# Graph attention on one core: units of six tiles instead of quads, one PSUM place for each product, sums copied by VectorE

## Chip, cores, metric

The kernel runs on one core of a Trainium2 chip. The metric is the device time of one execution in microseconds (us). The engines are named as in the profile: PE (TensorE; PEld is its weight load), DVE (VectorE), ACT (ScalarE), POOL (GpSimd), SP (SyncE).

## The reference

6250 nodes with 128 features, 206,250 edges sorted by receiver, with two sets of 32 edge features and a weight each. Everything is float32. `senders` is the input `src`, `receivers` is `dst`.

```python
w_ij = jax.nn.silu(edge_feats @ rad_W1 + rad_b1) @ rad_W2 + rad_b2
w_ij = w_ij + (jax.nn.silu(chi_scalar @ sph_W1 + sph_b1) @ sph_W2 + sph_b2)
q_i = (node_feats @ Wq).reshape(-1, 8, 16)[receivers]
k_j = (node_feats @ Wk).reshape(-1, 8, 16)[senders]
alpha = (q_i * w_ij * k_j).sum(axis=-1) / jnp.sqrt(16.0)
alpha = alpha * cutoffs[:, None]
v_j = (node_feats @ Wv)[senders].reshape(-1, 8, 16)
out = jax.ops.segment_sum(alpha[..., None] * v_j, receivers, num_segments=n_nodes) / 16.0
x = _layernorm(x + out.reshape(-1, 128), axis=-1)
```

## The kernel before

**Tiling.** 128 edges are a tile, four tiles a quad, four quads (16 tiles) a group. There are 1612 tiles, 403 quads and 101 groups. The receivers of a quad lie within 32 node rows, those of a group within 128.

**Start.** `load_nodes`, `turn` and `k_and_v` make keys and values of all nodes (x times Wk and Wv) and write them to a table in DRAM, `kv_tab`. Meanwhile GpSimd gathers rows of x for the first ten quads (`gather_x`, `XQ`), whose keys and values are computed directly. `tables`, `receivers` and others prepare row numbers.

**A quad in the main loop.** GpSimd gathers 128 rows of `kv_tab` per tile (`gathers`, line 131, through the helper at line 120), 14 quads ahead (`AHEAD`) into a ring of 16 (`RING`). TensorE computes the two hidden layers (`hidden_of`, line 405, tile `ph`), ScalarE applies silu (line 440, tile `act`); TensorE spreads the queries to the edges with a one-hot matrix (`q_at_edges`, line 413, `pq`) and computes the weights w_ij (`weigh`, line 447, `pw`: one product for the bias, line 450, then eight at line 455). VectorE multiplies queries by keys (`multiply`, line 463), by the weights (line 471), reduces over the head (473), scales (475), and multiplies the values (`messages`, 486). TensorE sums messages over the receivers of a quad with the one-hot matrix `hot` (`sum_quads`, line 492, `po`).

**A group.** `pick` and `turn_q` (line 378) fetch and transpose the x rows of the receivers, `make_q` (388) makes their queries; ScalarE copies both out of PSUM. `part_sums` (527) copies the sums of a group, `sum_group` (532 and 534) places them with the one-hot matrices `to` that `place` (521, 522) makes, and adds the rest of the group before (`tot`, copied at 536). `statistics` computes mean and variance (548 to 551), and every fourth group `roots` and `normalize` (556 to 570) finish rows, which SP writes.

**Order.** It is written out by hand: each engine runs its instructions in the program's order. The loop at line 624 takes a quad per turn, with TensorE one quad ahead of VectorE and the hidden layers two ahead. `ph`, `pq` and `pw` have two places in PSUM each (one bank a place), `po` and `side` one. `add_manual_dep` calls add waits: each gather waits for its own `pw` matmul of an earlier quad (line 137), and most steps of VectorE and ScalarE for marks of TensorE (`after`, `behind`). The last three quads are written out from line 681.

Of the kernel before, what the change touches and what calls it, by code (L numbers as in the profile page):

```python
# [44 lines left out]
XQ = 10  # L45
RING = 16
# [8 lines left out]
def gnn_kernel(ctx, tc, x, src, dst, weight, edges, rad_W1, rad_b1, rad_W2, rad_b2,  # L55
# [26 lines left out]
    src_x = const.tile([P, math.ceil(XQ / NQ) * GT], I32, name="src_x")  # L82
# [31 lines left out]
    alphas = side[:, 2 * P:2 * P + QT * HEADS].rearrange("p (t h) -> p t h", h=HEADS)  # L114

    def quad_of(name, bufs, width=D):
        return ep.tile([P, QT, width], F32, name=name, bufs=bufs)
# [8 lines left out]
    order = [g * NQ + j for g in range(NG) for j in (0, 2, 1, 3) if g * NQ + j < QUADS]  # L126
# [4 lines left out]
    def gathers(q, marks=()):  # L131

        kv = quad_of("kv", RING, 2 * D)
        for t in range(QT):
            o = gather(kv[:, t, :], kv_tab, src_i[:, q * QT + t:q * QT + t + 1])
            if marks:
                tc.add_manual_dep(o.ins, marks[t].ins.name, WAIT, reason="no gather ahead of TensorE")
        kv_of[q] = kv

    def load_feats(g, mark=None):  # L140
        feats_of[g] = gp.tile([P, EG // 2], F32, name="feats")
        o = nc.sync.dma_start(feats_of[g], edges[g])
        if mark is not None:
            tc.add_manual_dep(o.ins, mark.ins.name, WAIT, reason="one signal of TensorE a quad")
# [15 lines left out]
    def load_x(g, mark=None):  # L160
# [4 lines left out]
        o = nc.sync.dma_start(x_of[g].bitcast(U8), rows_from(x, r_of[g]))  # L165
        if mark is not None:
            tc.add_manual_dep(o.ins, mark.ins.name, WAIT, reason="one signal of TensorE a quad")
# [5 lines left out]
    nc.sync.dma_start(src_x, src[:, :math.ceil(XQ / NQ) * GT])  # L173
# [13 lines left out]
    with tc.tile_pool(name="nodes", bufs=1) as nodes, \  # L187
            tc.tile_pool(name="nodes_ps", bufs=2, space=PSUM) as nps:
        chunks = [(c, min(QT, NB - c)) for c in range(0, NB, QT)]
        quads_x = order[:XQ]  # L190
# [8 lines left out]
        def load_nodes(k):  # L199
            c, n = chunks[k]  # L200
            xs = ep.tile([P, EQ], F32, name="act", bufs=8).rearrange("p (t d) -> p t d", d=D)
            xs_of[k] = xs
# [8 lines left out]
        def gather_x(q):  # L211
            xs_of[q, "x"] = xs = quad_of("msg", XQ)
            for t in range(QT):
                gather(xs[:, t, :], x, src_x[:, q * QT + t:q * QT + t + 1])

        def turn(k, n):
            pt = nps.tile([P, QT, P], F32, name="pt", bufs=3)
            for i in range(n):
                nc.tensor.transpose(pt[:, i, :], xs_of[k][:, i, :], ident)
            xT_of[k] = nodes.tile([P, QT, P], F32, name="xT", bufs=4)  # L220
            nc.scalar.activation(xT_of[k][:, :n, :], pt[:, :n, :], AF.Copy)

        def k_and_v(k, n):
            kvs = quad_of("kv", RING, 2 * D)
            for h in range(0, n, 2):
                m = min(2, n - h)
                pk = nps.tile([P, 2, 2 * D], F32, name="pk", bufs=3)
                for i in range(m):
                    nc.tensor.matmul(pk[:, i, :], xT_of[k][:, h + i, :], wkv, start=True, stop=True)
                nc.vector.tensor_copy(kvs[:, h:h + m, :], pk[:, :m, :])  # L230
            return kvs
# [5 lines left out]

        qb = nodes.tile([P, NG, NQ], F32, name="qb")
# [82 lines left out]
        AHEAD = RING - 2  # L321
# [4 lines left out]
        for q in quads_x:  # L326
            gather_x(q)
# [7 lines left out]
        work = [(k, n) for k, (c, n) in enumerate(chunks)] + [((q, "x"), QT) for q in quads_x]  # L335
        turn(*work[0])
        turn(*work[1])
        for i, (k, n) in enumerate(work):
            if i + 2 < len(work):
                turn(*work[i + 2])  # L340
            kvs = k_and_v(k, n)
# [5 lines left out]
            store(k, kvs)  # L347
            if k + 8 < len(chunks):
                load_nodes(k + 8)
            if k == 4:  # L350
                nc.sync.dma_start(src_i, src)
            for f in beside.get(k, []):
                f()
            if i == len(chunks) - 1:
                nc.sync.dma_start(scale, weight)
        for q in order[XQ:AHEAD]:
            gathers(q)
# [5 lines left out]
        nc.vector.tensor_scalar(scale, scale, SCALE, None, op0=OP.mult)  # L363


    with tc.tile_pool(name="ps", bufs=1, space=PSUM) as pp:
# [8 lines left out]
        def turn_q(g):  # L375
            n = quads_in(g)
            pt = pp.tile([P, EQ], F32, name="pq", bufs=2)
            o = nc.tensor.matmul(pt[:, :n * W], x_of[g], pick_of[g][:, :n, :], start=True, stop=True)
            for m in made:
                tc.declare_no_dep(o.ins, m.ins, reason="VectorE has read it")  # L380
            xT_of[g] = gp.tile([P, P], F32, name="xT")
            return lambda: nc.scalar.activation(xT_of[g][:, :n * W], pt[:, :n * W], AF.Copy)

        def make_q(g):

            n = quads_in(g) * W
            pt = pp.tile([P, EQ], F32, name="pq", bufs=2)
            nc.tensor.matmul(pt[:n, :D], xT_of[g][:, :n], wq, start=True, stop=True)  # L388
            q_of[g] = gp.tile([P, D], F32, name="q")
            return lambda: nc.scalar.activation(q_of[g][:n, :], pt[:n, :D], AF.Copy)  # L390
# [12 lines left out]
        def hidden_of(q, i):  # L403

            g, j = divmod(q, NQ)
            r0, c0 = 2 * R * (j // 2) + i * R, EQ * (j % 2)
            act_of[q, i] = pp.tile([P, EQ], F32, name="ph", bufs=2)
            return nc.tensor.matmul(act_of[q, i], w1[r0:r0 + R, :],  # L408
                                    feats_of[g][r0:r0 + R, c0:c0 + EQ], start=True, stop=True)

        made = []

        def q_at_edges(q):
            g, j = divmod(q, NQ)
            b = slice(j * W, (j + 1) * W)
            pq_of[q] = pp.tile([P, EQ], F32, name="pq", bufs=2).rearrange("p (t d) -> p t d", d=D)
            made.clear()
            for t in range(QT):
                o = nc.tensor.matmul(pq_of[q][:, t, :], hotT_of[g][b, t * P:(t + 1) * P],  # L419
                                     q_of[g][b, :], start=True, stop=True)  # L420
                made.append(o)
            return o

        def after(o, mark, reason="one signal of TensorE a quad"):
            tc.add_manual_dep(o.ins, mark.ins.name, WAIT, reason=reason)

        def behind(o, marks, k):

            if marks:
                after(o, marks[k], "a signal of TensorE behind the quad's own")  # L430

        def first_layers(q):

            return [hidden_of(q, i) for i in range(2)][-1]

        def silus(q, mark, marks=()):

            for i in range(2):
                act = ep.tile([P, EQ], F32, name="act", bufs=8)
                o = nc.scalar.activation(act, act_of[q, i], AF.Silu, bias=b1[:, i:i + 1])  # L440
                if i == 0:
                    after(o, mark)
                else:
                    behind(o, marks, 0)
                act_of[q, i] = act

        def weigh(q):

            pw = pp.tile([P, EQ], F32, name="pw", bufs=2)
            nc.tensor.matmul(pw, onesb, brow.rearrange("p t d -> p (t d)"), start=True, stop=False)  # L450
            pw = pw_of[q] = pw.rearrange("p (t d) -> p t d", d=D)
            marks = []
            for t in range(QT):
                for i in range(2):
                    o = nc.tensor.matmul(pw[:, t, :], act_of[q, i][:, t * P:(t + 1) * P], w2[:, i, :],  # L455
                                         start=False, stop=(t == QT - 1 and i == 1))
                    marks.append(o)
            return marks

        def multiply(q, mark=None, t=slice(0, QT)):  # L460
            if t.start == 0:
                kq_of[q] = quad_of("kq", 3)
            o = nc.vector.tensor_tensor(kq_of[q][:, t, :], pq_of[q][:, t, :], kv_of[q][:, t, :D],  # L463
                                        op=OP.mult)
            if mark is not None:
                after(o, mark)

        def scores(q, t=slice(0, QT), marks=()):
            n = t.stop - t.start
            m = kq_of[q][:, t, :]  # L470
            nc.vector.tensor_tensor(m, pw_of[q][:, t, :], m, op=OP.mult)  # L471
            alpha = alphas[:, t, :]
            o = nc.vector.tensor_reduce(alpha, m.rearrange("p t (h e) -> p t h e", e=HD), AX.X, OP.add)  # L473
            behind(o, marks, 1)
            o = nc.vector.tensor_tensor(  # L475
                alpha, alpha,
                scale[:, q * QT + t.start:q * QT + t.stop, None].to_broadcast([P, n, HEADS]),
                op=OP.mult)
# [415 lines left out]
```

## Time and profile before

| | |
|---|---|
| median of 3 runs | 2040.4 us (2038.44 to 2041.47) |
| the profiled execution | 2041.07 us, span 2039.3 us |
| mean granted TensorE clock | 0.922 |
| gathers of `kv_tab`: count, mean duration | 1572, 947 ns |
| DVE operations 128x512 of the main loop, mean | 680 to 694 ns |
| silu 128x512 on ACT, mean | 685 ns |
| HBM read and written | 287.58 and 13.46 MB |

A line of a timeline gives start and duration in us, the engine, the line of the code, the operation, output and inputs with their shapes, the count, and in brackets the idle time of the engine before it and what ended it. A line of groups gives busy time and mean duration in ns, then the idle time before the instructions of the group and its releasers. A line of windows gives busy time of PE, PEld, DVE, ACT and POOL with the number of instructions, the granted clock, the busy share of the DMA engines and GB/s.

### The profile page before, as it was taken

The page shows a single profiled execution, that of the slowest core. Times are in us where ns is not written, and L with a number is a line of the kernel's source. Part 1 is how long each engine was busy: PE and PEld are TensorE (multiplying, and loading weights), DVE is VectorE, ACT ScalarE, POOL GpSimd, SP SyncE. Part 2 cuts the span into 40 slices and gives each one's busy share as a digit, 9 for nine tenths or more (in the row PEclk, how much of TensorE's full clock was granted, in tenths as well). Part 3 has the DMA queues.
Part 4 walks back from the last instruction along what each step waited for, and adds up shares of the span by engine and source line. Part 5 has one row for each costly group of instructions (what it writes and reads, how often), then busy time and mean ns, then how long its engine had stood idle before and what let it go on. Part 6 is the DMA issues. An engine that isn't in the chain of part 4 may idle for free.

```text
span 2039.3 us, 44163 instructions
## 1 busy us (share of the span) xinstructions
PE 1839.6 (90%) x16011; PEld 1525.5 (75%) x16011; DVE 1469.2 (72%) x3008; ACT 719.9 (35%) x1426; POOL 1527.4 (75%) x1620
## 2 busy tenths in 40 slices
PE   9899999898888988898988998889989989899897
PEld 7788887677777776777776776777767777777776
DVE  6688887687777666767777676767767676777677
ACT  2344433333333233333333333332333333333323
POOL 7777777777777777777777777777777777777775
PEclk9899999998898899988999889899999988898898
DMA  8455555455454445454454545454544545454543
GB/s 309 142 154 155 151 153 153 137 152 153 137 151 141 148 143 149 142 149 144 143 153 136 151 141 150 139 153 139 151 142 146 152 137 152 141 148 141 152 145 90
DMA packets 141371, 304.03 MB, mean 149 GB/s; under 512 B 34028, under 2 KB 73820, under 8 KB 141148
## 3 DMA queue, kind: packets, MB, share of 16 engines
q0 software_dynamic: 76736, 208.77, 35.9%
q1 hardware_dynamic: 62912, 92.00, 14.0%
q8 instruction: 127, 2.08, 0.4%
q14 instruction: 96, 0.79, 0.1%
q10 hardware_dynamic: 1500, 0.40, 0.1%
HBM read 287.58 MB, written 13.46 MB: 148 GB/s over the span
## 4 chain that ended last, share of the span: by engine, by line
PE 51%; DMA 20%; DVE 13%; issue 8%; ACT 4%; POOL 4%; DVEq 0%; POOLq 0%; ACTq 0%
PE pw L455 25%; DMA kv<-kv_tab,src_i 19%; PE pq L419 9%; PE ph L408 7%; DVE kq L463 5%; PE po L497 4%; DVE side L473 2%; POOL kv L120 2%; PE pw L450 2%; DVE kq L471 2%; POOL msg L120 2%; ACT L440 2%; ACT y L570 1%; PE pq L388 1%; PE pq L532 1%
## 5 line engine op out<-in xcount | busy, mean ns | idle before, releaser
L120 POOL DMA_INDIRECT kv<-kv_tab,src_i x1572 | 1488.0, 947 | 482.0 <-PE pw L455 188.9
L440 ACT ACTIVATE act<-ph,b 128x512 f32<-128x512 f32 x806 | 518.2, 685 | 1167.8 <-PE pq L419 1150.6
L455 PE MATMUL pw<-w,act 128*128 128x128 f32 x6448 | 906.1, 299 | 0.0
L455 PEld LDWEIGHTS pw<-w,act 128*128 128x128 f32 x6448 | 825.8, 208 | 102.2 <-issue 89.5
L463 DVE TENSOR_TENSOR kq<-pq,kv 128x512 f32<-128x512 f32 x404 | 278.1, 688 | 394.3 <-DMA kv<-kv_tab,src_i 240.0
L408 PE MATMUL ph<-feats,w 32*128 32x512 f32 x1612 | 505.4, 685 | 21.9 <-ACT act L440 21.9
L419 PE MATMUL pq<-q,hotT 32*128 32x128 f32 x3224 | 498.1, 297 | 23.5 <-DVE kq L463 23.0
L419 PEld LDWEIGHTS pq<-q,hotT 32*128 32x128 f32 x3224 | 419.6, 199 | 81.7 <-issue 51.6
L473 DVE TENSOR_REDUCE side<-kq 128x32 f32<-128x512 f32 x404 | 280.2, 694 | 42.0 <-PE pw L455 0.5
L486 DVE TENSOR_TENSOR msg<-kv,side 128x512 f32<-128x512 f32 x404 | 277.5, 687 | 43.8 <-DVE side L475 1.4
L471 DVE TENSOR_TENSOR kq<-pw,kq 128x512 f32<-128x512 f32 x404 | 274.7, 680 | 0.1
L408 PEld LDWEIGHTS ph<-feats,w 32*128 32x128 f32 x1612 | 139.6, 195 | 104.5 <-issue 59.3
L450 PE MATMUL pw<-brow,onesb 3*128 3x512 bf16 x403 | 160.4, 398 | 0.0
L497 PE MATMUL po<-msg,hot 128*32 128x128 f32 x3200 | 156.6, 293 | 0.0
L532 PE MATMUL pq<-part,to 128*128 128x128 f32 x200 | 46.1, 313 | 105.0 <-DVE kq L463 66.9
L532 PEld LDWEIGHTS pq<-part,to 128*128 128x128 f32 x200 | 30.6, 193 | 118.0 <-issue 69.8
L475 DVE TENSOR_TENSOR side<-side,scale 128x32 f32<-128x32 f32 x404 | 80.8, 200 | 42.9 <-DVE side L473 1.4
L497 PEld LDWEIGHTS po<-msg,hot 128*32 128x32 f32 x3200 | 71.8, 112 | 38.6 <-issue 5.0
L388 PE MATMUL pq<-wq,xT 128*128 128x128 f32 (+1 forms) x202 | 47.8, 322 | 32.2 <-DVE kq L463 31.6
L394 DVE TENSOR_TENSOR hotT<-relb,side 128x512 f32<-128x512 bf16 x101 | 68.8, 681 | 0.0
L399 DVE TENSOR_TENSOR hot<-rel,side 128x512 f32<-128x512 f32 x100 | 66.1, 661 | 0.0
L388 PEld LDWEIGHTS pq<-wq,xT 128*128 128x128 f32 (+1 forms) x202 | 35.3, 218 | 40.3 <-DVE kq L463 39.6
(101 smaller groups left out, 831.0 us busy)
## 6 DMA issues: line engine op xcount, KB each, us to landing
feats<-in_edges SPq DMA_DIRECT2D x101, 512.0 KB
kv<-kv_tab,src_i POOLq DMA_INDIRECT x1572
relb<-rel_lin SPq DMA_DIRECT2D x101, 128.0 KB
x<-in_x SPq DMA_DIRECT2D x101, 64.0 KB
out<-y SPq DMA_DIRECT2D x101, 64.0 KB
kv_tab<-kv SPq DMA_DIRECT2D x12, 512.0 KB
act<-in_x SPq DMA_DIRECT2D x12, 256.0 KB
dst_i<-in_dst SPq DMA_DIRECT2D x1, 808.0 KB
```

What stands on the lines that cost most here:

```text
L120: return nc.gpsimd.indirect_dma_start(out=o, out_offset=None, in_=table, in_offset=bass.IndirectOffsetOnAxis(ap=index, axis=0))
L388: nc.tensor.matmul(pt[:n, :D], xT_of[g][:, :n], wq, start=True, stop=True)
L408: return nc.tensor.matmul(act_of[q, i], w1[r0:r0 + R, :], feats_of[g][r0:r0 + R, c0:c0 + EQ], start=True, stop=True)
L419: o = nc.tensor.matmul(pq_of[q][:, t, :], hotT_of[g][b, t * P:(t + 1) * P], q_of[g][b, :], start=True, stop=True)
L440: o = nc.scalar.activation(act, act_of[q, i], AF.Silu, bias=b1[:, i:i + 1])
L450: nc.tensor.matmul(pw, onesb, brow.rearrange("p t d -> p (t d)"), start=True, stop=False)
L455: o = nc.tensor.matmul(pw[:, t, :], act_of[q, i][:, t * P:(t + 1) * P], w2[:, i, :], start=False, stop=(t == QT - 1 and i == 1))
L463: o = nc.vector.tensor_tensor(kq_of[q][:, t, :], pq_of[q][:, t, :], kv_of[q][:, t, :D], op=OP.mult)
L471: nc.vector.tensor_tensor(m, pw_of[q][:, t, :], m, op=OP.mult)
L473: o = nc.vector.tensor_reduce(alpha, m.rearrange("p t (h e) -> p t h e", e=HD), AX.X, OP.add)
L486: o = nc.vector.tensor_tensor(msg_of[q][:, t, :].rearrange("p t (h e) -> p t h e", e=HD), kv_of[q][:, t, D:].rearrange("p t (h e) -> p t h ...
L497: o = nc.tensor.matmul(po_of[g][j * W:(j + 1) * W, :], hot_of[g][:, j * QT + t, :], msg_of[g * NQ + j][:, t, :], start=(t == 0), stop=(t = ...
```

## The change

A unit takes the place of the quad: a quad and half of another one, six tiles. Three quads `a, b, c` of a hand-made order become two units: `a` with the first half of `b`, and `c` with the second half. 269 units cover the 1612 tiles. VectorE's five steps and the gathers go by units; the ring has ten units of kv (60 tiles; before 16 quads, 64 tiles), gathered nine units ahead.

Each product of a unit has its own place in PSUM: `ph` three banks (two layers of the unit's own quad and one of a shared quad), `pq` two (six tiles, `turn_q` and `make_q`), `pw` two (six tiles, the sums of a group and its total). There is one place of each. `behind` makes the first instruction that writes a bank again wait for the bank's last reader.

The first gather of a unit waits for `weigh` of an earlier unit (`past`), the other five do not. The manual waits of VectorE, ScalarE and SP are gone. Four small results of a group (`xT`, `q`, `part`, `tot`) are copied from PSUM by VectorE, not by ScalarE. The sums over the edges of a group are done in one unit (`sums`), the total in the next (`closes`); `place` is a task at the end of the unit of `sums`. `scale` is written in the order of units by 25 small operations. The end of the kernel is written out anew for the last two units.

```diff
-XQ = 10
-RING = 16
+U = 6
+XU = 7
+RING = 10
...
-    order = [g * NQ + j for g in range(NG) for j in (0, 2, 1, 3) if g * NQ + j < QUADS]
+    turn_of_quads = ((0, 0), (0, 1), (0, 2), (1, 0), (0, 3), (1, 2), (1, 1), (2, 0), (1, 3), (2, 1), (2, 2), (2, 3))
+    order = [(b + g) * NQ + j for b in range(0, NG, 3) for g, j in turn_of_quads if (b + g) * NQ + j < QUADS]
+    order[-7:] = [*range((NG - 2) * NQ, (NG - 1) * NQ), QUADS - 1, QUADS - 3, QUADS - 2]
+    units = []
+    for a, *rest in (order[i:i + 3] for i in range(0, len(order), 3)):
+        units.append([a * QT + t for t in range(QT)])
+        if rest:
+            b, c = rest
+            units[-1] += [b * QT, b * QT + 1]
+            units.append([c * QT + t for t in range(QT)] + [b * QT + 2, b * QT + 3])
+    UNITS = len(units)
+    layers = [[(unit[0] // QT, 0), (unit[0] // QT, 1)] for unit in units]
+    for v in range(1, UNITS, 2):
+        b = units[v][-1] // QT
+        layers[max(v - 2, 0)].append((b, 0))
+        layers[v - 1].append((b, 1))
...
+    group_of = [[t // GT for t in unit] for unit in units]
+    first = [min(v for v in range(UNITS) if g in group_of[v]) for g in range(NG)]
+    last = [max(v for v in range(UNITS) if g in group_of[v]) for g in range(NG)]
+    place_of = {t: (v, k) for v, unit in enumerate(units) for k, t in enumerate(unit)}
...
+
+    def gathers(v, mark=None):
+
+        kv = unit_of("kv", RING, 2 * D)
+        for k, t in enumerate(units[v]):
+            o = gather(kv[:, k, :], kv_tab, src_i[:, t:t + 1])
+            if mark is not None and k == 0:
+                tc.add_manual_dep(o.ins, mark.ins.name, WAIT, reason="no gather ahead of TensorE")
+        kv_of[v] = kv
...
-        AHEAD = RING - 2
+        AHEAD = RING - 1
...
-        nc.vector.tensor_scalar(scale, scale, SCALE, None, op0=OP.mult)
+        full = UNITS // 8 * 8
+        for v in list(range(8)) + list(range(full, UNITS)):
+            for k in range(0, len(units[v]), QT):
+                m = min(QT, len(units[v]) - k)
+                i, t = v * U + k, units[v][k]
+                o, w = scale[:, i:i + m], weights[:, t:t + m]
+                if v < 8:
+                    o, w = (a[:, :full * U].rearrange("p (c t) -> p c t", t=8 * U)[:, :, b:b + m]
+                            for a, b in ((scale, i), (weights, t)))
+                nc.vector.tensor_scalar(o, w, SCALE, None, op0=OP.mult)
...
-        def turn_q(g):
+        def turn_q(g, ps):
...
-            pt = pp.tile([P, EQ], F32, name="pq", bufs=2)
+            pt = ps[:, U * D:(U + 1) * D]
...
-        def make_q(g):
+            return o, lambda: nc.vector.tensor_copy(xT_of[g][:, :n * W], pt[:, :n * W])
...
+        def behind(o, *banks):
+
+            for bank in banks:
+                if bank in readers:
+                    after(o, readers.pop(bank), "a bank has one user at a time")
...
+        def q_at_edges(v, part):
+            for k in part:
+                t = units[v][k]
+                g, j = divmod(t // QT, NQ)
+                b = slice(j * W, (j + 1) * W)
+                o = nc.tensor.matmul(tiles_in(pq_of[v], v)[:, k], hotT_of[g][b, t % QT * P:(t % QT + 1) * P],
+                                     q_of[g][b, :], start=True, stop=True)
+                behind(o, "pq%d" % (k // QT))
+
+        def hidden(s, v=None):
+
+            ph = pp.tile([P, 3, EQ], F32, name="ph", bufs=1)
+            for k, (q, i) in enumerate(layers[s][:3]):
+                if v is not None and k == 2:
+                    q_at_edges(v, range(QT))
+                hidden_of(ph, k, q, i)
+            if v is not None:
+                q_at_edges(v, range(len(layers[s][:3]) // 3 * QT, len(units[v])))
+            return ph
...
+        def silu(ps, k, q, i):
+            act = ep.tile([P, EQ], F32, name="act" if k < 2 else "act_b", bufs=4)
+            readers["ph%d" % k] = nc.scalar.activation(act, ps[:, k, :], AF.Silu, bias=b1[:, i:i + 1])
...
+        def weigh(v):
+
+            n = len(units[v])
+            for k in range(0, n, QT):
+                m = min(QT, n - k) * D
+                o = nc.tensor.matmul(pw_of[v][:, k * D:k * D + m], onesb,
+                                     brow.rearrange("p t d -> p (t d)")[:, :m], start=True, stop=False)
+                behind(o, "pw%d" % (k // QT))
...
+        def multiply(v):
+            kq_of[v] = unit_of("kq", 2)
+            n = len(units[v])
+            o = nc.vector.tensor_tensor(kq_of[v][:, :n], tiles_in(pq_of[v], v), kv_of[v][:, :n, :D],
+                                        op=OP.mult)
+            readers["pq0"] = readers["pq1"] = o
+
+        def weigh_scores(v):
+            m = kq_of[v][:, :len(units[v])]
+            o = nc.vector.tensor_tensor(m, tiles_in(pw_of[v], v), m, op=OP.mult)
+            readers["pw0"] = readers["pw1"] = o
...
+        def part_sums(g, po):
+            return nc.vector.tensor_copy(part_of[g][:n, :], po[:n, :])
...
+        def sum_group(g, ph, bank):
             n, part, to = quads_in(g) * W, part_of[g], to_of[g]
-            ph = pp.tile([P, EQ], F32, name="pq", bufs=2)
-            nc.tensor.matmul(ph[:, :D], to[:n, 0, :], part[:n, :], start=True, stop=(g == 0))
+            o = nc.tensor.matmul(ph, to[:n, 0, :], part[:n, :], start=True, stop=(g == 0))
+            behind(o, bank)
...
+        def totals(g, ph):
+            nc.vector.tensor_copy(tot_of[g], ph)
+            return add_x(g, ph)
...
+        turns = {first[g] - 2: g for g in range(1, NG)}
+        makes = {first[g] - 1: g for g in range(1, NG)}
+        sums = {last[g] + 2: g for g in range(G - 1)}
+        closes = {last[g] + 3: g for g in range(G - 1)}
+        for g in range(NG):
+            if first[g] - 4 >= 0:
+                at(first[g] - 4, lambda g=g: pick(g))
+            if g < G:
+                at(first[g] + 2, lambda g=g: one_hots(g))
+                at(min(last[g] + 2, UNITS - 3), lambda g=g: place(g))
+            if g < G - 1:
+                at(last[g] + 3, lambda g=g: statistics(g))
...
+        for v in range(UNITS - 2):
+            pq_of[v] = pp.tile([P, 2 * EQ], F32, name="pq", bufs=1)
+            after_q, after_w = [], []
+            for at_v, f in ((turns, turn_q), (makes, make_q)):
+                if v in at_v:
+                    o, copy = f(at_v[v], pq_of[v])
+                    behind(o, "pq1")
+                    after_q.append(copy)
+            ph = hidden(v + 1, v)
+            pw_of[v] = pp.tile([P, 2 * EQ], F32, name="pw", bufs=1)
+            small = [pw_of[v][:, (U + k) * D:(U + k + 1) * D] for k in range(2)]
+            if v in sums:
+                g = sums[v]
+                sum_quads(g, small[0], "pw1")
+                after_w.append(lambda g=g: part_sums(g, small[0]))
+            if v in closes:
+                g = closes[v]
+                sum_group(g, small[1], "pw1")
+                after_w.append(lambda g=g: totals(g, small[1]))
+            if v == judged:
+                after_w.append(verdict(pw_of[v]))
+            past, mark = mark, weigh(v)
+            silus(v + 1, ph)
+            if v + AHEAD < UNITS:
+                gathers(v + AHEAD, past)
+            multiply(v)
+            for f in after_q:
+                readers["pq1"] = f()
+            if v in makes:
+                one_hots_T(makes[v])
+            weigh_scores(v)
+            for f in after_w:
+                readers["pw1"] = f()
+            messages(v, scores(v))
+            for f in tasks.get(v, []):
+                f()
+            write_rows()
```

More of the change, by code (lines that the diff above doesn't have):

```diff
@@ L129, in gnn_kernel, with tiles_in, load_feats @@
     po_of, part_of, to_of, tot_of, xT_of, y0_of, kq_of, pick_of, pq_of, pw_of = ({} for _ in range(10))
[L131 to L144, printed above, removed]
+    def tiles_in(ps, v):
+        return ps.rearrange("p (t d) -> p t d", d=D)[:, :len(units[v])]
+    def gathers(v, mark=None):
[5 more added lines that the diff above has]
+        kv_of[v] = kv
+    def load_feats(g):
+        feats_of[g] = gp.tile([P, EG // 2], F32, name="feats", bufs=3)
+        nc.sync.dma_start(feats_of[g], edges[g])
     def quads_in(g):
@@ L424, in after @@
[L424 to L478, printed above, removed]
-            behind(o, marks, 2)
-            return alpha
@@ L482, in messages @@
[L482 to L498 removed]
+        readers = {}
@@ L560, in normalize @@
         def normalize(a, b, sd):
[L561 to L562 removed]
+            start, n = first_of(a), b - a
+            y0, mv = y0_of[start]
             rs = gp.tile([P, LB], F32, name="rs")
@@ new lines, in gnn_kernel @@
+        for i, f in enumerate(checks):
+            at(first[CHECK] + 2 * i, f)
+        judged = next(v for v in range(first[CHECK] + 2 * len(checks) + 1, UNITS)
+                      if v not in sums and v not in closes)
+        for i in range(3):
+            at(first[G - 2] + i, lambda q=G * NQ + (0, 2, 1)[i]: wide_one_hots(q))
+        at(first[G - 1], lambda: place(G))
+        for g in range(2):
+            pick(g)
+        ph = hidden(0)
+        for g in range(1, 3):
+            load_feats(g)
+            load_x(g)
@@ new lines, in gnn_kernel @@
+        multiply(a)
+        part_sums(G - 1, end[:, 0, :D])
+        pq_of[b] = pp.tile([P, 2 * EQ], F32, name="pq", bufs=1)
+        q_at_edges(b, range(QT))
+        sum_group(G - 1, end[:, 1, :D], "ph1")
+        weigh_scores(a)
+        pw_of[b] = pp.tile([P, 2 * EQ], F32, name="pw", bufs=1)
+        weigh(b)
+        sd = roots(G - 3, G - 1)
+        normalize(G - 3, G - 1, sd)
+        write_rows()
+        messages(a, scores(a))
+        totals(G - 1, end[:, 1, :D])
+        moments(G - 1)
@@ new lines, in gnn_kernel @@
+        for t in wide:
+            if place_of[t][0] == a:
+                sum_wide(po, t)
+        nc.tensor.matmul(po, to_of[G][:, 1, :], tot_of[G - 1], start=False, stop=False)
+        write_rows()
+        sd = roots(G - 1, G)
+        multiply(b)
+        normalize(G - 1, G, sd)
+        write_rows()
+        weigh_scores(b)
+        messages(b, scores(b))
+        for t in units[b]:
+            sum_wide(po, t, stop=(t == units[b][-1]))
+        add_x(G, po)
+        moments(G)
+        sd = roots(G, G + 1)
```

366 lines of the change are left out of this document (148 added, 218 removed).

## The prediction

> **What bounds the kernel now.** I read the shares of busy time first, then the costliest groups, then GpSimd's own timeline, because the share alone misleads here. Parts 1 and 5 of the page:
>
> ```profile
> PE 1839.6 (90%) x16011; PEld 1525.5 (75%) x16011; DVE 1469.2 (72%) x3008; ACT 719.9 (35%) x1426; POOL 1527.4 (75%) x1620
> ...
> L120 POOL DMA_INDIRECT kv<-kv_tab,src_i x1572 | 1488.0, 947 | 482.0 <-PE pw L455 188.9
> ```
>
> PE is busiest, but POOL's 482.0 us of idle over 1572 gathers is 0.307 us each, and the next view shows that this is no waiting. GpSimd's timeline (start, duration, what, idle before and its releaser):
>
> ```profile
> 3.03 1.10 POOL L120 DMA_INDIRECT msg<-in_x,src_x  x1 [1.42 <-DMA src_x<-in_src]
> 4.43 0.94 POOL L120 DMA_INDIRECT msg<-in_x,src_x  x1 [0.30 <-issue]
> 5.68 0.94 POOL L120 DMA_INDIRECT msg<-in_x,src_x  x1 [0.30 <-issue]
> ...
> 73.22 0.95 POOL L120 DMA_INDIRECT kv<-kv_tab,src_i  x1 [0.30 <-issue]
> 77.49 0.94 POOL L120 DMA_INDIRECT kv<-kv_tab,src_i  x1 [3.33 <-PE pw L455]
> 78.74 0.95 POOL L120 DMA_INDIRECT kv<-kv_tab,src_i  x1 [0.31 <-PE pw L455]
> ```
>
> The second to eighth gathers, which the program gives no wait at all, have the same 0.30 us pause as those with a wait for TensorE. From the 57th gather (77.49) to the 1612th (2022.38) there are 1555 steps in 1944.89 us: 1.2507 us each, unbroken. So GpSimd sets the time: 3.03 to 2022.38 us with one stall (3.0 us), then a tail of 16.9 us to the span's end, 2039.3. The profiled execution took 2041.07, so 1.8 us lie around the span; the median, 2040.4, is 0.7 lower.
>
> How much slower could the other engines become? Windows (PE, PEld, DVE, ACT, POOL busy, granted clock, DMA, GB/s):
>
> ```profile
> 100.00:500.00 400.00, 374.07 (x3534) 315.82 (x3527) 320.73 (x657) 157.52 (x312) 302.67 (x320) 0.95 0.52 151
> 500.00:900.00 400.00, 357.49 (x3125) 294.79 (x3124) 282.94 (x582) 138.88 (x275) 302.65 (x320) 0.92 0.50 146
> ```
>
> 16011 matmul records over 403 quads are 39.7 a quad. In the first window PE did 3534/39.7 = 89 quads, one in 4.5 us: it was eating the 14 quads gathered ahead. Later it does one in 5.0, GpSimd's pace. Per group of 16 tiles: GpSimd 16 x 1.2507 = 20.0 us, the rest 18.0. The slack is 2 us in 20, and the verdict hangs on whether the change spends it.
>
> PE's clock belongs to that slack. PE's timeline:
>
> ```profile
> 1000.37 0.46 PE L532 MATMUL pq<-part,to 128*128 128x128 f32 x2 [1.81 <-DVE kq L463]
> ...
> 1003.58 3.78 PE L455 MATMUL pw<-w,act 128*128 128x128 f32 x16
> ...
> 1009.57 2.05 PE L455 MATMUL pw<-w,act 128*128 128x128 f32 x16
> ```
>
> Some 1 us after a wait of 1.81 us the same 16 matmuls take 3.78 instead of 2.05 us; one-us windows show a granted clock of 0.50 from about 1001.5 to 1008.2. That stretch lost 3.4 us of TensorE work.
>
> **The change part by part.** All sums are per group (2.667 units).
>
> *GpSimd's waits.* Five of six gathers lose their wait for TensorE. By the rows above the pause does not depend on it, so this is worth 0. The number of gathers stays 1612 (42 of x instead of 40), the cadence too. A unit's first gather now also waits for `messages` of the unit ten earlier, with five gathers queued behind it; this only matters if VectorE is ten units late.
>
> *TensorE's work at full clock.* Hidden layers, q at the edges and bias: 1008.30 to 9.57 is 1.27 a quad, x4 = 5.1. A unit has a second, half-width bias product: half of the 0.30 from one bias to the first `pw`, 0.15 x 2.667 = 0.4. `pw`: 1.89 to 1.98 a quad (1013.22 to 15.11, 1009.57 to 11.55), x4 = 7.7. Sums over edges: 0.58 + 0.35 + 0.35 = 1.3. `sum_group` 0.61, `turn_q` 0.32, `make_q` 0.42. Sum 15.8, and 15.4 of it was there before.
>
> *The new wait.* Before, `pq`, `pw` and `ph` each had two turns, and `place` ran a group early. Now each product has one place, and `sum_group(g)` stands in PE's queue between q at the edges and the bias of a unit, while the `to` that it reads is made by `place(g)` in the unit just before, behind its `messages`. Count from the end of that unit's last `pw` matmul. PE does `turn_q` 0.32, hidden layers and q about 1.5: it is at `sum_group` at 1.8. VectorE can only then begin `weigh_scores`. A 128x256 operation takes 0.42 and a 128x512 one 0.69, so 128x768 is 0.96 (estimate from these rows); a dependent operation starts 0.10 after the last ends, an independent one 0.08 before. 0.2 to start, 0.9 `weigh_scores`, 0.2 copy of `part`, 1.06 reduction, 0.3 scaling, 0.9 `messages`, 0.6 for two `to` (0.34 each): 4.2. PE waits 4.2 - 1.8 = 2.4 us, once a group, and behind it stand the unit's bias and `pw`, for which `weigh_scores` waits in turn. Bounds: 0 if GpSimd paces everything (the wait then fills idle time), 2.9 if each of the five hand-overs costs 0.1 more. I take 2.4. The ScalarE chain of square roots cost PE 2.17 + 1.14 us before 1040.85 and 1043.24, every fourth group: 0.8 a group, kept. Together 3.2.
>
> *The clock.* Loss is (1 - clock) x time: 0.05 x 18 = 0.9 in the first window, 0.08 x 20 = 1.6 in the second. In the changed kernel a stretch without `pw` is longer (hidden layers of three, six q's, two biases, and the wait of 2.4, against 1.3 to 2.9 with waits before). I take 1.5; bounds 0.9 and 3.4 (one stretch like that at 1001.5 in each group).
>
> [...]
>
> *Copies from ScalarE to VectorE.* Four a group (0.27 to 0.28 each on ScalarE; a 128x128 copy on VectorE took 0.295): VectorE gets 1.1 us. Its five big steps shrink from 4 x 3.2 = 12.8 to 2.667 x 4.2 = 11.2. With 3.4 of small work it is busy below 15 of 20 us: no bound by itself. ScalarE, 35% busy, gains nothing that anybody waits for.
>
> *Loads.* SP's DMAs keep their number (101 of each) and lose marks; they are issued groups ahead, so 0. If that cover were gone, a late load would delay one group in 101 by its few us.
>
> *Start and end.* `scale` becomes 25 small operations instead of one of 0.98 us: at 0.15 to 0.3 each (rows of 128x4 to 128x128) some 5 us, so the first `multiply` moves from 73.1 to about 78. From the last `multiply` to the end: 0.6 + 0.4 + 0.6 + 0.8 + 0.3 + 0.7 for the last quad and then 6.8 as from 2032.5 to 2039.3: 10 us.
>
> *Sum.* 15.8 + 3.2 + 1.5 = 20.5 us a group, above GpSimd's 20.0: 7.69 a unit. 78 + 268 x 7.69 + 10 = 2149, plus 1.8 around the span: **2150 us**. GpSimd then waits for `messages`, unit after unit.
>
> **The rivals.**
>
> 1. *GpSimd still paces.* If the clock costs under 1.0 us a group (15.8 + 3.2 + 1.0 = 20.0), the waits sink into idle time. For it: the first window lost 0.9. Against: longer stretches without `pw`. The 61st gather, due at 79.5, waits for the first `messages`, about 85 (7 us after `multiply`): a stall of 5.5 instead of 3.0. The tail is about 1.5 shorter. 2041.1 + 2.5 - 1.5 = 2042 us.
> 2. *The clock oscillates each group.* One stretch like that at 1001.5 a group: 15.8 + 3.2 + 3.4 = 22.4, 8.4 a unit, 78 + 2251 + 12 = 2341. For it: the wait of 2.4 exceeds the 1.81 that sufficed. Against: waits of 1.4 to 2 in the trace were often without effect. [...]
> 3. *The other side: the pause is the wait.* If 0.30 us were the price of a wait on GpSimd, five of six would go: 1570 x 5/6 x 0.30 = 392 us off its chain, and the rest would pace; faster than before from under 20.0 us a group on, at full clock 19.0: 78 + 268 x 7.13 + 12 = 2000. Against it stand the gathers without any wait and with the same 0.30.
>
> **How the numbers follow.** About 0.2% (4 us) is what a measurement here can tell from no change. Chances: forecast 0.64; rival 1 0.19 (0.16 within 0.2%, 0.02 slower, 0.01 faster); rival 2 0.11; rival 3 0.06. Faster 0.07, same 0.16, slower 0.77. The range goes from rival 1 with its shorter tail and no longer stall (2037) to a clock loss of 2.3 us a group (21.3, 2230); rivals 2 and 3 and a little of the forecast are outside. The forecast's own range is 2075 to 2230.
>
> **What would show it.** GpSimd: gaps still 0.30 where nothing is late, but once a unit a wait of the order of 0.2 to 3 us on VectorE's `msg`. PE: about 2.4 us before `pw<-part,to`, released by `to`. Clock at or below 0.92 and a tail of some 70 us after the last gather, since ten units are then still to be done. Wrong would be: an unbroken 1.25 us cadence (rival 1), a pause below 0.3 (rival 3), a mean clock near 0.85 (rival 2).

## The result and the profile after

The changed kernel takes 2204.57 us (median of 5 runs, 2204.45 to 2205.52), the kernel before 2039.92 (5 runs, 2038.44 to 2041.47): ratio 1.0809, 95% interval 1.0793 to 1.0825. The forecast, 2150, had the direction and the place, the wait at the end of each group; of the 165 us it had 110, and it put the clock's cost at no more than before. The mean granted clock went from 0.922 to 0.847.

First the costliest groups of the page (busy us, mean ns | idle before, releaser), as for the kernel before:

```profile
L121 POOL DMA_INDIRECT kv<-kv_tab,src_i x1570 | 1484.6, 946 | 585.8 <-issue 548.6
...
L569 PE MATMUL pw<-part,to 128*128 128x128 f32 x198 | 67.2, 438 | 137.3 <-DVE to L559 137.3
```

GpSimd's gathers cost what they did (946 ns against 947) but it now idles 585.8 us (482.0 before). TensorE stands 137.3 us in front of `sum_group`'s first product, and what releases it is the `to` of `place`. The kernel before had idle time there too, with another releaser:

```profile
L532 PE MATMUL pq<-part,to 128*128 128x128 f32 x200 | 46.1, 313 | 105.0 <-DVE kq L463 66.9
```

There GpSimd's unbroken steps set the pace, so that idle time did not bound the kernel. New is that `to` comes late, and that the pace is TensorE's. The list of waits (total us, times, longest) gives the count, and the square-root chain's share:

```profile
PE pw L569 <- DVE to L559: 137.3, 82, 2.5
...
PE ph L447 <- ACT act_b L473: 83.8, 26, 4.5
```

A close is the unit in which `sum_group` runs. 82 of 99 closes wait, 1.58 us in the median. TensorE's timeline at two closes, with an undisturbed unit between them (start, duration, what, idle before and its releaser):

```profile
1003.43 0.77 PE L569 MATMUL pw<-part,to 128*128 128x128 f32 x2 [1.87 <-DVE to L559]
...
1005.30 3.78 PE L490 MATMUL pw<-w,act 128*128 128x128 f32 x16
1008.88 1.57 PE L490 MATMUL pw<-w,act_b 128*128 128x128 f32 x8
...
1013.96 2.05 PE L490 MATMUL pw<-w,act 128*128 128x128 f32 x16
1015.84 1.06 PE L490 MATMUL pw<-w,act_b 128*128 128x128 f32 x8
...
1020.61 0.77 PE L569 MATMUL pw<-part,to 128*128 128x128 f32 x2 [1.57 <-DVE to L559]
...
1022.48 3.78 PE L490 MATMUL pw<-w,act 128*128 128x128 f32 x16
```

The `pw` behind each of these two waits takes 3.78 us for 16 records, that of the unit between 2.05: half clock (the trace grants 0.50 from 1003.12 to 1009.94 us). A unit's 24 records take 2.95 us at full clock; behind 65 of the 81 waits over 0.5 us they took more than 4. VectorE's timeline ahead of the first close shows what made `to` late:

```profile
999.76 0.96 DVE L504 TENSOR_TENSOR kq<-pw,kq 128x768 f32<-128x768 f32 x1 [1.42 <-PE pw L490]
1000.63 0.28 DVE L565 COPY part<-pw 128x128 f32<-128x128 f32 x1
1000.83 0.95 DVE L510 TENSOR_REDUCE side<-kq 128x48 f32<-128x768 f32 x1
...
1002.07 0.95 DVE L520 TENSOR_TENSOR msg<-kv,side 128x768 f32<-128x768 f32 x1
1002.94 0.34 DVE L559 TENSOR_SCALAR to<-side,rowq 128x128 f32<-128x128 f32 x1
```

`part` was there at 1000.91; `to`, which needs nothing of this unit, stands behind the whole unit's scores and messages and ends at 1003.28. Windows (PE, PEld, DVE, ACT, POOL busy, granted clock, DMA, GB/s) show the same clock all along:

```profile
100.00:500.00 400.00, 358.47 (x2978) 293.27 (x2976) 262.76 (x490) 115.34 (x185) 292.42 (x310) 0.84 0.48 141
500.00:900.00 400.00, 355.59 (x2965) 290.61 (x2965) 260.03 (x506) 114.65 (x185) 284.75 (x302) 0.84 0.47 136
```

And GpSimd, at the 60th and 61st gather:

```profile
78.01 0.95 POOL L121 DMA_INDIRECT kv<-kv_tab,src_i  x1 [0.30 <-issue]
86.85 0.94 POOL L121 DMA_INDIRECT kv<-kv_tab,src_i  x1 [7.89 <-issue]
88.10 0.95 POOL L121 DMA_INDIRECT kv<-kv_tab,src_i  x1 [0.30 <-issue]
```

One long stall, then the same 0.30 us pause, now with five of six gathers waiting for nothing.

### The profile page after: what moved, and what is told of

The parts are those of the page before. It is cut to its first block, busy times and chain, and to the rows that moved or that the text cites. A ratio compares the mean times of both kernels' runs of the same rounds, so it can differ in the third digit from the quotient of the medians.

```text
span 2202.7 us, 41001 instructions
## 1 busy us (share of the span) xinstructions
PE 1961.7 (89%) x16151; PEld 1604.1 (73%) x16151; DVE 1436.0 (65%) x2758; ACT 629.8 (29%) x1027; POOL 1526.1 (69%) x1620
## 4 chain that ended last, share of the span: by engine, by line
PE 57%; DVE 14%; POOL 7%; issue 7%; DMA 7%; ACT 5%; DVEq 0%; POOLq 0%; ACTq 0%
PE pw L490 34%; POOL kv L121 7%; DMA kv<-kv_tab,src_i 7%; PE ph L447 6%; PE pq L456 5%; PE pw L485 5%; DVE kq L504 4%; DVE side L510 3%; PE pw L569 3%; PE pw L533 2%; DVE msg L520 2%; PE pw L572 2%; ACT L473 2%; ACT act L473 1%; ACT y L613 1%
## 5 line engine op out<-in xcount | busy, mean ns | idle before, releaser
L121 POOL DMA_INDIRECT kv<-kv_tab,src_i x1570 | 1484.6, 946 | 585.8 <-issue 548.6
L490 PEld LDWEIGHTS pw<-w,act 128*128 128x128 f32 x4304 | 643.6, 237 | 124.5 <-issue 124.5
L490 PE MATMUL pw<-w,act 128*128 128x128 f32 x4304 | 704.1, 331 | 0.0
L473 ACT ACTIVATE act<-ph,b 128x512 f32<-128x512 f32 x538 | 340.1, 683 | 1262.9 <-PE ph L447 1262.6
L504 DVE TENSOR_TENSOR kq<-pw,kq 128x768 f32<-128x768 f32 x269 | 256.9, 955 | 623.4 <-PE pw L490 620.1
L447 PE MATMUL ph<-feats,w 32*128 32x512 f32 x1612 | 566.2, 671 | 84.2 <-ACT act_b L473 83.8
L490 PE MATMUL pw<-w,act_b 128*128 128x128 f32 x2144 | 335.9, 309 | 0.0
L490 PEld LDWEIGHTS pw<-w,act_b 128*128 128x128 f32 x2144 | 321.7, 230 | 0.0
L498 DVE TENSOR_TENSOR kq<-pq,kv 128x768 f32<-128x768 f32 x269 | 255.3, 949 | 74.5 <-PE ph L447 60.2
L520 DVE TENSOR_TENSOR msg<-kv,side 128x768 f32<-128x768 f32 x269 | 256.2, 952 | 9.5
L510 DVE TENSOR_REDUCE side<-kq 128x48 f32<-128x768 f32 x269 | 256.1, 952 | 2.4
L569 PE MATMUL pw<-part,to 128*128 128x128 f32 x198 | 67.2, 438 | 137.3 <-DVE to L559 137.3
L473 ACT ACTIVATE act_b<-ph,b 128x512 f32<-128x512 f32 x268 | 184.3, 688 | 2.2 <-PE ph L447 2.2
```

Of the source, the lines that this page charges most:

```text
L121: return nc.gpsimd.indirect_dma_start(out=o, out_offset=None, in_=table, in_offset=bass.IndirectOffsetOnAxis(ap=index, axis=0))
L447: o = nc.tensor.matmul(ph[:, k, :], w1[r:r + R, :], feats_of[g][r:r + R, c:c + EQ], start=True, stop=True)
L473: readers["ph%d" % k] = nc.scalar.activation(act, ps[:, k, :], AF.Silu, bias=b1[:, i:i + 1])
L490: o = nc.tensor.matmul(tiles_in(pw_of[v], v)[:, k], act_of[t // QT, i][:, t % QT * P:(t % QT + 1) * P], w2[:, i, :], start=False, stop=(i ...
L498: o = nc.vector.tensor_tensor(kq_of[v][:, :n], tiles_in(pq_of[v], v), kv_of[v][:, :n, :D], op=OP.mult)
L504: o = nc.vector.tensor_tensor(m, tiles_in(pw_of[v], v), m, op=OP.mult)
```

## The experiments

The runs of this section were made in other jobs than the two above, and there the kernel before itself took 2599 to 2621 us on each chip. The second group below shows part of what is different there; the third takes it away.

**First job: place early, fill the wait, copies back, one wait a quad.**

`e1_place_early`:
```diff
-                at(min(last[g] + 2, UNITS - 3), lambda g=g: place(g))
+                at(min(last[g] + 1, UNITS - 3), lambda g=g: place(g))
```


> The changed kernel with place(g) one unit earlier, so that `to` is there a unit before sum_group reads it. Theory A (the wait for `to` at every close, and the half clock that follows it, set the pace): the 137 us of waiting before pw<-part,to are gone, the granted clock rises from 0.847 to 0.91 or more, a group costs TensorE 15.8 + 0.8 + 1.0 to 1.6 = 17.6 to 18.2 us, so GpSimd's 20.0 pace again: 2036 to 2050 us. Rival B (the clock falls because each product has one place and stretches without pw are long, whatever is waited for): clock stays at 0.87 or below, a loss of about 3 us a group remains, 19.6 to 20.5 us a group: 2045 to 2150. Rival C (VectorE's longer queue, or GpSimd's waits, are what costs): stays within 10 us of 2204.

`e2_fill_wait`:
```diff
             if v in closes:
                 g = closes[v]
+                for i in range(12):
+                    o = nc.tensor.matmul(small[1], ident, ident, start=True, stop=True)
+                    behind(o, "pw1")
                 sum_group(g, small[1], "pw1")
```


> The changed kernel with place(g) where it was, and 12 more products of 128x128 (about 1.5 us at full clock, results overwritten) in TensorE's queue right ahead of sum_group: the wait for `to` keeps its end, but TensorE works through it. Theory A with the clock as the larger part: pw after a close takes 2.05 us for 16 instead of 3.78, clock at 0.92 or above, a group costs 15.8 + 1.4 + 0.8 + 1.0 to 2.0 = 19.0 to 20.0 us: GpSimd paces or nearly so, 2036 to 2060 us. Rival W (the waiting itself costs, the half clock only falls into it): 2180 to 2215, whatever the clock shows. Rival B (long stretches without pw lower the clock): clock stays below 0.88, time 2180 to 2230.

`e3_copies_scalar` (the other three copies likewise; a bank then has two readers to wait for):
```diff
-            return nc.vector.tensor_copy(part_of[g][:n, :], po[:n, :])
+            return nc.scalar.activation(part_of[g][:n, :], po[:n, :], AF.Copy)
```


> The changed kernel with the four copies a group (xT, q, part, tot) back on ScalarE. Theory A: VectorE bounds nothing by itself; the copy of part leaves the chain ahead of `to`, so the wait for `to` may shrink by 0.2 to 0.3 us a group, the half clock stays: 2175 to 2207 us, clock 0.84 to 0.86. Rival C (the copies on VectorE cost their 1.1 us a group): 2204 - 110 = about 2095.

`e4_before_one_wait`, on the kernel before:
```diff
-            if marks:
+            if marks and t == 0:
                 tc.add_manual_dep(o.ins, marks[t].ins.name, WAIT, reason="no gather ahead of TensorE")
```


> The kernel before with GpSimd's explicit wait for TensorE on the first gather of a quad only (three of four waits removed, nothing else changed). Theory A: the pause between gathers does not come from the wait: 0.30 us stays in front of gathers with and without one, 1.25 us a gather, 2040 us within 4. Rival 3 of the prediction (the pause is the price of the wait): 1570 x 3/4 x 0.30 = 353 us off GpSimd's chain, TensorE's 18 us a group pace instead: 1990 or below.

Measured: 3244.1, 3155.0, 2994.8 and 2590.0 us, the kernel before 2599.3 in the same job. No theory foretold such times, so as times they decide nothing. The first was run again on another chip, and the changed kernel itself on a third:

> The kernel of e1_place_early once more, since that job's chip ran even the kernel before in 2599 us instead of 2040, with stalls on TensorE and ScalarE that no engine released. Theory A (the wait for `to` at every close, and the half clock behind it, set the pace): waiting before pw<-part,to gone, clock 0.91 or more, GpSimd paces: 2036 to 2050 us. Rival B (one place for each product and long stretches without pw lower the clock by themselves): clock 0.87 or below, 2045 to 2150. Rival C (VectorE's longer queue or GpSimd's waits): within 10 us of 2204.

> The changed kernel itself, unaltered, as the yardstick for the experiments, because in the jobs so far the kernel before took 2599 us instead of 2040. If this job is like those: TensorE's instructions come 0.7 us apart for some 11 us once every 256 instructions or so, and the changed kernel lands near the 3243 us of the version with place(g) early, since those bursts and not the wait for `to` set the pace; theory A then expects waits of 1.4 to 1.9 us before pw<-part,to at the closes outside the bursts, which the version with place(g) early doesn't have. If the job is undisturbed: 2204 us against 2040.

3243.0 us (before 2599.5) and 3059.8 us (before 2618.7): the disturbance stays, and hits the version with `place` early more than the changed kernel.

One thing is clear all the same, from e4. Of its 1571 gaps between gathers 1264 are under 0.5 us, and all but three of these are 0.30 to 0.31, 91 with an explicit wait for TensorE and the rest without. The third rival of the prediction is out; the profile after shows the same. The time of e4, ratio 0.9965 (0.9948 to 0.9982), agrees but says less, since GpSimd idles 977.6 us there, mostly for other reasons.

For the rest I read the closes that the disturbance did not touch (no two TensorE instructions 0.7 or 1.4 us apart from 9 us before `sum_group` to the end of its `pw`). Half clock means more than 4 us for the 24 records of `pw`, where 2.95 is full:

| kernel | such closes | half clock behind | of all 99, half clock behind |
|---|---|---|---|
| e6, the changed kernel | 63 | 43 | 69 |
| e3, copies on ScalarE | 75 | 49 | 69 |
| e1 and e5, `place` early | 12 and 15 | 2 and 1 | 6 and 6 |
| e2, wait filled | 37 | 1 | 51 |

The numbers of undisturbed closes move by a few with how widely "0.7 or 1.4" is taken. At the 62 disturbed closes of e2 the half clock can come from the disturbance, so e12 below is the cleaner test of filling.

So the half clock follows the idling, not the unit's layout: the order of the unit's own products is the same in all of them, and in e2 `to` is as late as before. Copies on ScalarE change nothing in it. One size was wrong in e2: a product leaves two records, and 12 of them took 2.94 us instead of 1.5, longer than the wait.

**Second group: what disturbs.** In e5 GpSimd's and TensorE's timelines, put side by side (GpSimd first):

```profile
1023.17 0.94 POOL L121 DMA_INDIRECT kv<-kv_tab,src_i  x1 [9.14 <-PE ph L447]
1024.42 0.95 POOL L121 DMA_INDIRECT kv<-kv_tab,src_i  x1 [0.30 <-issue]
...
1036.96 0.95 POOL L121 DMA_INDIRECT kv<-kv_tab,src_i  x1 [0.30 <-issue]
1049.21 0.95 POOL L121 DMA_INDIRECT kv<-kv_tab,src_i  x1 [11.30 <-issue]
```

```profile
1028.16 0.95 PE L533 MATMUL pw<-msg,hot 128*32 128x128 f32 x25
1029.51 0.27 PE L533 MATMUL pw<-msg,hot 128*32 128x128 f32 x1 [0.39 <-issue]
1030.24 0.28 PE L533 MATMUL pw<-msg,hot 128*32 128x128 f32 x1 [0.46 <-issue]
...
1038.72 0.37 PE L490 MATMUL pw<-w,act 128*128 128x128 f32 x1 [0.82 <-issue]
1040.12 3.35 PE L490 MATMUL pw<-w,act 128*128 128x128 f32 x14 [1.03 <-issue]
```

Twelve gathers run unbroken from 1023.17 to 1037.91. About 5.6 us after the first one TensorE begins to take its instructions 0.7 or 1.4 us apart, waiting for nothing that the profile names, and is free again 2.2 us after the last. There are some 110 to 120 such stretches in e5, 8 to 9 us each in the mean (the count depends on where one ends and the next begins). The recorded runs of both kernels have none, with gathers just as unbroken.

These stretches are not all of it. On TensorE e4 has fewer than twenty, and yet it takes 550 us more than the kernel before in the first recording. In its list of waits ScalarE and VectorE stand for signals that the profile gives to no instruction of this core ("remote"):

```profile
ACT act L440 <- remote: 624.8, 91, 9.4
DVE kq L463 <- remote: 485.3, 96, 6.7
```

The recorded runs of both kernels have no such wait; e6, the changed kernel, has 236 on all its engines. To test whether runs of gathers are the cause, each gather was put behind another instruction of TensorE (e8; e7 also has `place` early):

```diff
-                gathers(v + AHEAD, past)
+                gathers(v + AHEAD, past and [past, q_marks[-1], *(pw_marks[-12:][i] for i in (1, 4, 7, 11))])
```

`e9_before_spread`, on the kernel before:
```diff
-                    gathers(order[i + AHEAD], old[-QT:])
+                    gathers(order[i + AHEAD], [old[-1], mark, marks[2], marks[-1]])
```

> place(g) one unit early, as in e5, and each of the six gathers of a unit behind another instruction of TensorE (the last pw of the unit before, the last q of this one, then the 2nd, 5th, 8th and 12th pw product), so that GpSimd can't run twelve gathers in a row. Theory S (in these jobs TensorE's instructions come 0.7 us apart, and its signals late, from about the sixth unbroken gather until 2.2 us after the last): no such stretches, and theory A then holds for the rest: no wait for `to`, clock 0.90 or more, 17.6 to 18.2 us a group for TensorE, GpSimd or its new waits pace: 2040 to 2300 us. If S falls: about 3243, as without the spreading.

> The changed kernel with the same spreading, place(g) where it was. Theories S and A together: waits of 1.4 to 1.9 us before pw<-part,to at the closes, half clock behind most of them, about 21 us a group: 2190 to 2350 us, and 80 to 160 us more than e7. Rival B or C (place is not the point): e7 and e8 within 30 us. If S falls: about 3060.

> The kernel before with the four gathers of a quad spread in the same way (behind the last pw of the quad before, the last q of this one, and its 3rd and last pw). Theory S: the late signals vanish, 2040 to 2200 us instead of 2600. If S falls: 2580 to 2620.

2758.1, 2704.7 and 2567.4 us, before 2621.1. Spreading takes 485 us from the version with `place` early (3243.0), 355 from the changed kernel (3059.8; the kernel before took 2599.5 to 2621.1 on these chips, 0.8% apart) and 2.1% (1.9 to 2.4%) from the kernel before. Theory S is borne out in direction and misses every range; e7 still has some 65 to 90 stretches of 3 to 4 us. At the closes all is as theory A has it (half clock behind 2 of all 99 closes in e7, behind 68 in e8), yet e7 is not faster than e8 but 53 us slower. In these jobs something other than the closes sets the time.

**Third job: no gathers.** Without them, from the tenth unit on, there is neither GpSimd's pace nor the disturbance; the result is then another than the reference's:

```diff
+        if v >= AHEAD:
+            kv_of[v] = kv_of[v % AHEAD]
+            return
         kv = unit_of("kv", RING, 2 * D)
```

e11 adds the edit of e1, e12 that of e2 with 6 products.

> The changed kernel with the gathers of kv left out from the tenth unit on (each unit multiplies by the rows of one of the first nine units instead, so the result is another): GpSimd neither paces nor disturbs, what is left is the pace of TensorE, VectorE and ScalarE alone. Theory A: that pace is what the changed kernel showed at 2204.6 us, about 21.0 us a group: 2180 to 2215 us, with waits of 1.4 to 1.9 us at the closes and a clock near 0.85. Rival B' (part of the 21.0 was GpSimd's transfers slowing the others): below 2150.

> The same, with place(g) one unit earlier. Theory A: wait and half clock at the closes both go, 15.8 + 0.8 + 1.0 to 1.6 = 17.6 to 18.2 us a group: 78 + 268 x 6.6 to 6.83 + 10 = 1857 to 1918 us, clock 0.91 or more. Only the wait matters, not the clock (W): 21.0 - 1.4 = 19.6 us a group, 2058 us. Neither (B, C): within 20 us of e10.

> The kernel without the gathers, place(g) where the change has it, and 6 products of 128x128 (12 records of 0.128 us, 1.5 us; results overwritten) ahead of sum_group: the wait is filled, not removed. Theory A with the clock as a term of its own: 15.8 + 1.5 + 0.8 + 1.0 to 1.6 = 19.1 to 19.7 us a group: 2008 to 2068 us, clock 0.91 or more. Only the wait matters (W): as e10, within 20 us.

Measured: 2254.7, 1913.2 and 2102.9 us. The first and third are 40 and 35 us above their ranges because the start, which still gathers, is disturbed: the first `multiply` begins at 127.8 to 129.7 us, at 78.6 in the changed kernel. Each of the three has eight "remote" waits, 71 to 89 us in all, all before 107 us; the last gather ends at some 104. After that there is none, and no stretch of TensorE as above. From first to last `multiply`, in us per 16 tiles:

| | changed kernel | e10 | e11, `place` early | e12, wait filled |
|---|---|---|---|---|
| us per 16 tiles | 21.04 | 21.07 | 17.63 | 19.59 |
| expected | 20.5 (prediction) | 21.0 | 17.6 to 18.2 | 19.1 to 19.7 |

e10 is the changed kernel's pace to 0.2%, so that pace never came from gathers. Its wait and clock are the changed kernel's too, and e11 loses both (waits of e10; then the windows of e10 and of e11 from 1000 us):

```profile
PE pw L572 <- DVE to L562: 137.4, 82, 2.5
```

```profile
1000.00:1400.00 400.00, 355.38 (x3005) 290.85 (x3005) 260.16 (x495) 116.67 (x188) 0.00 (x0) 0.85 0.12 37
```

```profile
1000.00:1400.00 400.00, 379.79 (x3567) 309.05 (x3564) 307.65 (x585) 137.59 (x222) 0.00 (x0) 0.94 0.14 45
```

3567 matmul records instead of 3005 in the same 400 us. And a close of e12, where `to` is as late as ever but TensorE works meanwhile:

```profile
1003.21 1.60 PE L725 MATMUL pw<-ident 128*128 128x128 f32 x12
1004.76 0.49 PE L572 MATMUL pw<-part,to 128*128 128x128 f32 x2
...
1005.87 2.05 PE L493 MATMUL pw<-w,act 128*128 128x128 f32 x16
```

The 12 records fill 1.55 us, the `pw` behind runs at full clock, and the kernel with more work is 1.48 us per 16 tiles faster than e10. This rules out that only the wait costs (W), and that VectorE's queue, the copies or single PSUM places set the pace by themselves (B, C): they are the same in e10, e11 and e12.

## Why the prediction was right, and which term was mis-sized

The forecast's sum per 16 tiles beside what the runs show. The waits are totals over 99 closes; the work is e11's 17.63 less its wait and its clock loss, (1 - 0.94) x 17.63 = 1.1, with the clock of its windows from 500 to 1400 us:

| term | forecast | changed kernel |
|---|---|---|
| TensorE at full clock | 15.8 | 15.8 (17.63 - 0.76 - 1.1) |
| wait for `to` | 2.4 | 137.3 / 99 = 1.39 |
| square-root chain | 0.8 | 83.8 / 99 = 0.85 |
| clock | 1.5 | 21.04 - 15.8 - 1.39 - 0.85 = 3.0 |
| sum | 20.5 | 21.04 |

- **The clock is the term that was mis-sized.** I took 1.5, near the kernel before, with bounds of 0.9 and 3.4; it is 3.0, and (1 - 0.847) x 21.04 = 3.2 by the granted clock. 1.1 of it is there without the wait (e11). The other 2 come with it: e10 to e11 is 3.44, of which the wait is 1.39 and the rest, 2.05, the half clock. The closes themselves show nearly that: from `sum_group`'s first product to the end of `pw` it is 6.30 us in the mean behind the changed kernel's 81 waits over 0.5 us, and 4.01 in the median of e11, so 81 / 99 x 2.29 = 1.9. I had seen waits of 1.4 to 2 us without effect in the trace of before and let them speak against one slow stretch a group. Behind the closes four of five waits of that size (65 of 81) had one, and their length does not tell which.
- **The wait is smaller than its sum.** 1.58 us in the median instead of 2.4. The working counted both `to` tiles (0.6); the first product needs one, and from the start of `weigh_scores` to the end of that `to` it is 3.52 us. At 17 closes there is no wait, because the square-root chain has held TensorE up just before; the clock is half there too (the 24 records of `pw` take 5.27 to 5.49 us). The two errors partly cancel, -1.0 and +1.5, and that is luck: with the clock at 3.0 and the wait as forecast the sum would be 22.0 a group, some 2300 us (an estimate by the prediction's own sum), outside its range.
- **Rival 2 had the mechanism and the mean clock of 0.85**, which the prediction had named as the sign that its own account is wrong. In time it was too dear at 2341: it priced one 3.4 us loss on top of a wait of 2.4. In the changed kernel half clock followed waits from 1.51 us up, shorter ones than the 1.81 that I had read in the trace of before.
- **Rival 1** (GpSimd still paces) needed a clock loss under 1.0 and falls. Rival 3 falls by e4 and by the 0.30 us pause after.
- **Start and end** were right: first `multiply` at 78.6 (78 said), 10.0 us from the last to the end (10 said). 78.6 + 268 x 7.8886 + 10.0 = 2202.7, the span. The 0.20 us per unit between 7.69 and 7.889 are 53 of the 55 us missing.
- **Signs.** The tail after the last gather is 77.3 us (some 70 said). GpSimd does not wait once a unit: there are 42 gaps over 0.5 us, 2.3 in the median, 120 in all. Its ten units of store let it run on at 1.25 us and stop seldom.
- **Nothing for GpSimd's waits, the copies and the loads** holds as far as it was tested: the gaps of e4 for the first; for the others e10 and e11, where the same copies and loads allow 21.07 and 17.63, so they don't hold the units to more than 17.63. None of them was priced alone in an undisturbed run.

**What stays open.** e11's 17.63 is below GpSimd's 20.0, so with `place` one unit earlier the units should be paced by GpSimd again, near rival 1's 2042 us (an estimate). It wasn't run beside a kernel before of 2040 us, and the disturbed runs (e1, e5, e7) can't show it; no version here that computes the reference is shown to beat the kernel before.

## What to carry to other kernels

When a product gets a single place or a task a new slot, look for the small operand that is made late: `to` needs nothing of its unit and stood behind the whole unit. Price a wait of TensorE as the idle time plus what runs at half clock behind it; here the second was the larger (some 2 against 1.39 us a group). To tell the two apart, fill the wait with products whose results are thrown away.

## What the runs showed of the hardware

Idle spells of TensorE of 1.58 us in the median were followed by half clock on 65 of 81 occasions. Filled with 128x128 products (e12) they were not: the 16 slow closes left there and the 17 left in e11 all have another idle spell of over 1 us in the 8 us before, in all but two of them the square-root chain's.

In the trace of the changed kernel 65 of the 93 stretches at 0.50 are 6.83 us long, the one from 1003.12 to 1009.94 us among them. The length of a wait does not tell whether half clock follows: the 65 waits with it are 1.51 to 2.50 us long, the 16 without it 1.57 to 1.92. In the kernel before two waits of 1.81 us in front of `sum_group` came out both ways: the 16 records of `pw` behind the one that ends at 1000.37 took 3.78 us, those behind the one that ends at 1560.98 took 2.05. What else counts was not tested.

The pause of 0.30 us between indirect gathers is the same with and without a wait: in e4 all but three of the 1264 gaps under 0.5 us are 0.30 to 0.31, 91 with an explicit wait for TensorE and the rest without.

In e5 TensorE's instructions came 0.7 or 1.4 us apart from some 5.6 us after the first of an unbroken row of gathers until 2.2 us after the last (the row from 1023.17 us; some 110 to 120 such stretches). Other engines stood for signals that the profile gives to no instruction of this core (in e4 ScalarE 91 times, 624.8 us). In e10 to e12, whose last gather ends at some 104 us, neither is found after 107 us. In the two recorded profiles gathers ran unbroken without this. What differs between the jobs is not known.
